# Second-norm tiles of six more blocks turned through DRAM, and images turned at the read in a transformer-block kernel

## The chip, the cores and the metric

The kernel runs on one core of a Trainium2 chip. The metric is device time in microseconds; three runs of the kernel before took 3532.73, 3537.45 and 3537.84 us, median 3537.45. A core has TensorE (PE, matmuls, with its weight loads shown apart as PEld), VectorE (DVE), ScalarE (ACT), GpSimd (POOL) and SyncE (SP). Nearly all DMAs of this kernel are issued by SP, in order, and are carried by sixteen DMA engines.

## The reference

One adaLN transformer block in float32 over x of shape (8, 1024, 512), 16 heads of 32, with a condition vector for each batch:

```python
mod = silu(condition) @ Wada + bada
sh_a, sc_a, gt_a, sh_m, sc_m, gt_m = split(mod, 6, axis=1)
xm = layernorm(x, g1, be1) * (1 + sc_a) + sh_a
x = x + gt_a * (causal_attention(xm, Wqkv) @ Wproj + bproj)
xm = layernorm(x, g2, be2) * (1 + sc_m) + sh_m
x = x + gt_m * (gelu(xm @ W1 + b1) @ W2 + b2)
```

W1 is 512 x 2048. The attention is causal over 1024 tokens.

## The kernel before

The 8 x 1024 tokens are cut into 16 blocks of 512: block n is half n % 2 of batch n // 2. Each block passes through: load and first norm (tile `hat_a`), the turned and modulated operand `xm_a` and its sums `t_a`, the projections k, q, v, attention, the output projection (`Wproj`), the second norm (`hat_m`, `xm_m`, `t_m`), and the MLP, `up` and `down`. The linear layers use a seven-product scheme of Strassen's kind, so that sums of operands and of weights are formed on DVE and POOL. All matmuls are float32 and go out as groups of four, one for each 32 columns of the array (`matmul`, L217). Weights come in 256 KB pieces through a ring of eight tiles `w` (`fetch`, L358 to L362), fetched ahead in the order of use.

**Windows.** `plan[w]` lists the linear steps that run beside the attention of block w: rest of the MLP of block w - 2, v of w, `proj` and `mt` of n = w - 1 (`mt` builds `xm_m` of n), then k, v or q of w + 1, then the first `up` products of n. So the second norm of an odd block n runs beside the attention of the even block n + 1.

**Attention.** Odd blocks, and the even ones up to 2, are attended with the keys along partitions: scores twice, exponentials from ACT, totals on POOL (L1854). The even blocks from 4 on are attended by rows (`attend_rows`), in ten units a block. In a unit, PE makes scores with queries along partitions, DVE takes maxima, ACT the exponentials `rows_p` (128 partitions x 2048 floats), and DVE turns every 32 x 32 piece of it. What is left is a permutation of whole 32-row bands, and that is done by DRAM: `spread_unit` writes the tile to a DRAM tile `image` (L2060) and reads it back as a page `turned` (L2076), from which PE multiplies with v (L2092). Raw tiles and pages share three SBUF slots. A unit's page is read when its image is written, a slot is free and the page before has been asked for.

**Turning a norm's tile.** `modulated` makes an operand with channels along partitions out of the normalized tile (tokens along partitions). For keys in the set `by_pe` PE transposes sixteen 128 x 128 pieces into PSUM banks (L778) and DVE or ACT move them out with gain and shift (L782, L788). For all others `turn` does as for images: DVE turns 32 x 32 pieces (L714), one 1 MB DMA writes `held` to DRAM (L723), four DMAs of 256 KB read it back into the tile (L728), and gain and shift are applied from SBUF. In the kernel before, `by_pe` holds the first norms of blocks 0 and 1 and the second norms of blocks 0, 1, 14, 15 and of 3, 5, 7, 9, 11 and 13. All `hat` tiles share one buffer.

**The order of work.** The program is written out as one static order for each engine by a planner in Python. It keeps model clocks (`now`), the time at which each thing will be there (`written`) and be free (`left`), and always goes on with the thread that waits least by these. DMAs are modelled by `note_dma(ns)`: 425 ns on SP for the issue, then 1000 ns until it begins or the end of the DMA before, then ns, then 1200 ns to land:

```python
        begun = max(now["SP"], due(reads, ()), after)
        now["SP"] = begun + ISSUE
        now["DMA"] = max(begun + BEGIN, now["DMA"]) + ns
        for k in writes:
            written[k] = now["DMA"] + LAND
```

At run time the engines wait on semaphores; the planner's times fix only the order. SP carries DMAs on eight semaphores in turn, and the rows below show it waiting for an earlier, unrelated DMA before it issues the next.

Of the kernel before, what the change touches and what calls it, by code (L numbers as in the profile page):

```python
# [9 lines left out]
F32 = mybir.dt.float32  # L10
# [12 lines left out]
def kernel(  # L23
# [33 lines left out]
    nc = tc.nc  # L57
    B, T, D = x.shape
    HD = W1.shape[1]
    P = 128  # L60
    hd = D // H
    scale = float(hd) ** -0.5
    TB = 512
    NTT = TB // P
# [18 lines left out]
    kept = ctx.enter_context(tc.tile_pool(name="kept", bufs=1, space=bass.MemoryType.DRAM))  # L83
# [7 lines left out]
    NB = len(blocks)  # L91
# [3 lines left out]
    written, left = {}, {}  # L95
# [9 lines left out]
    def due(reads=(), writes=()):  # L105
        t = 0.0
        for k in reads:
            t = max(t, written.get(k, 0.0))
        for k in writes:
            t = max(t, left.get(k, 0.0))  # L110
        return t

    def note(engine, ns, reads=(), writes=(), port=False):
        start = max(now[engine], due(reads, writes))
        if port:
            start = max([start] + [b for a, b in pool_spans if a <= start < b])
        end = start + ns
        now[engine] = end
        if engine == "POOL":
            pool_spans.append((start, end))  # L120
            del pool_spans[:-16]
        for k in reads:
            left[k] = max(left.get(k, 0.0), end + SYNC)
        for k in writes:
            written[k] = end + SYNC
        return end

    def note_dma(ns, reads=(), writes=(), after=0.0):
# [7 lines that stand above are left out]
    def note_pe(ns, form, reads=(), writes=()):  # L136
        now["PE"] = max(now["PE"], due(reads, writes))
        if shape[0] != form:
            shape[0] = form
            now["PE"] += SWITCH  # L140
        note("PE", ns, reads)
        spent[0] += ns
        for k in writes:
            written[k] = now["PE"] + PIPE
# [98 lines left out]
    def mlp_steps(n):  # L243
        return [("u", n, i) for i in range(NQ)] + [("d", n, part) for part in range(4)]
# [9 lines left out]
    for w in range(1, NB):  # L254
        n = w - 1
        m = mlp_steps(n)
# [29 lines left out]
    n = NB - 1  # L286
# [102 lines left out]
    rows = tmp.tile([P, TB], F32, tag="y", name="rows")[:n_rows, :P]  # L389
# [4 lines left out]
        r0 += n  # L394
    O_G1, O_BE1, O_G2, O_BE2, O_BPROJ, O_B2, O_B1, O_BADA = at

    by_pe = ({"a0", "a1", "m0", "m1", f"m{NB - 2}", f"m{NB - 1}"}) | {f"m{n}" for n in range(3, NB - 1, 2)}
    Q = P // NTT

    def hat_tile(key):  # L400
        return tmp.tile([P, NTT, D], F32, tag="hat", name=f"hat_{key}", bufs=1)

    def load_x(n):
        b, h = blocks[n]
        rows = hat_tile(f"a{n}")
        written["hat free"] = NEVER
        for t in range(NTT):
            some = x[b, h * TB + t * P : h * TB + (t + 1) * P, :]
            if f"a{n}" in by_pe:
                nc.sync.dma_start(rows[:, t, :], some)  # L410
            else:
                nc.sync.dma_start(rows[ts(t, Q), :, :], some.rearrange("(t i) d -> i t d", i=Q))
            note_dma(3600, [], [("x", f"a{n}")])
        return rows

    x_pre = {0: load_x(0)}
    fetch()

# [134 lines left out]
    def add_job(job, reads, first=False):  # L553

        at = sum(1 for other in jobs if other[2]) if first else len(jobs)
        jobs.insert(at, (job, reads, first))
# [149 lines left out]
    def turn(key, rows, xm):  # L706

        small_blocks = xm.rearrange("p c n -> p (c n)")
        by_tile = small_blocks.rearrange("p (m h t i) -> p h m t i", m=NTT, h=NC, t=NTT)
        written["blocks", key] = NEVER  # L710

        def turn_tile(t):
            into = by_tile[:, :, :, t, :]
            nc.vector.transpose(into, rows[:, t, :].rearrange("p (h m i) -> p h m i", m=NTT, i=Q))  # L714
            done = [("blocks", key)] if t == NTT - 1 else []
            note("DVE", 620, [("hat", key, t)], done)

        for t in range(NTT):
            add_job(lambda t=t: turn_tile(t), [("hat", key, t)], key[0] == "m")
        yield [("blocks", key)], []  # L720
        held = kept.tile([P, NTT * D], F32, tag=f"held_{turns[0] % 2}", name=f"held_{key}")
        turns[0] += 1
        nc.sync.dma_start(held, small_blocks)  # L723
        note_dma(2600, [("blocks", key)], [("held", key)])
        yield [("held", key)], []
        for m in range(NTT):
            some = held[:, ts(m, D)].rearrange("(a i) d -> i a d", i=Q)
            nc.sync.dma_start(rows[ts(m, Q), :, :], some)  # L728
            note_dma(1250, [("held", key)], [("turned", key)])
        yield [("turned", key)], []  # L730

# [3 lines left out]
    def modulated(key, gain, shift, b, guards):  # L735
# [23 lines left out]
        if turned:  # L759
            yield from turn(key, got, xm)  # L760
# [923 lines left out]
    def take_slot():  # L1684
        slot = free_p.pop(0)
        count_slots()
        return slot

    def give_slot(slot):
        free_p.append(slot)  # L1690
        count_slots()
# [362 lines left out]
    def spread_unit(n, raw, slot, parts, i):  # L2054

        yield [("p", slot)], []
        image = kept.tile([P, NTT, TB], F32, tag=f"image_{i % 5}", name=f"image_{n}_{i}")
        for a in range(NTT):
            into = image[:, a, :].rearrange("(b x) r -> x b r", x=hd)
            nc.sync.dma_start(into, raw[ts(a, hd)].rearrange("x (b r) -> x b r", b=NTT))  # L2060
            note_dma(700, [("p", slot)], [("image", n, i)])
        left["p", slot] = now["DMA"] + LAND
        written["image", n, i] += 1500
        raws.remove(slot)
        give_slot(slot)
        while True:
            yield [("image", n, i), SLOT, ("paged", n, i - 1)], []
            if free_p and len(pages) < 9:
                break
        taken_slot = take_slot()  # L2070
        pages.append(taken_slot)
        key = ("p", taken_slot)
        yield [], [key]
        written["paged", n, i] = 0.0
        page = pp.tile([P, NTT, TB], F32, tag=f"p{taken_slot}", name=f"turned_{n}_{i}")
        nc.sync.dma_start(page, image)  # L2076
        note_dma(2700, [("image", n, i)], [key])
        written[key] += 2000
        if i:
            yield [("valued rows", n, i - 1)], []  # L2080
        for qt, kh, c0, w, gg in parts:
            first = (n, gg) not in row_outs
            for k in range(w // P):
                yield [key, ("v", n), ("v done", n)], ["po"] if first and k == 0 else []
                if first and k == 0:
                    row_outs[n, gg] = [ps_po.tile([P, TB], F32, tag="o", name=f"po_{n}_{gg}"), 0]
                out = row_outs[n, gg]
                out[1] += 1
                for j in range(HPG):
                    r = slice(j * hd, (j + 1) * hd)  # L2090
                    at = c0 + k * P + j * hd
                    nc.tensor.matmul(  # L2092
                        out[0][r, ts(qt, P)],
                        vs[n][:, k, gg * P + j * hd : gg * P + (j + 1) * hd],
                        page[:, :, at : at + hd],
                        start=out[1] == 1,
                        stop=out[1] == 10,
                        skip_group_check=True,
                    )
                note_pe(2 * COLUMN * P, "columns", [key], ["po"])  # L2100
            if out[1] == 10:
                finish_rows(n, gg, out[0])
        pages.remove(taken_slot)
        give_slot(taken_slot)
        written["valued rows", n, i] = 0.0
# [27 lines left out]
    def finish_rows(n, g, out):  # L2133

        into = qTs[n][:, g, :]
        if wait_of(([("inverses", n, g)], [])) > 0 or max(now["DVE"], due(["po"])) > max(now["ACT"], due(["po"])) + 2500:
            nc.scalar.copy(into, out)
            note_act(585, None, ["po"], [("values", n, g)])
            start(scaled(n, g, into))
        else:  # L2140
            nc.vector.tensor_tensor(into, out, inverse_rows.pop((n, g)), ALU.mult)
            note("DVE", 690, ["po", "top"], [("att", n)])
            finished(n, g)
# [112 lines left out]
```

## Time and profile before

| | |
|---|---|
| median of three runs | 3537.45 us |
| profiled execution | 3537.05 us, span 3535.2 us |
| PE busy | 3398.7 us (96%) |
| DVE, POOL, ACT busy | 2287.1, 1790.1, 1249.8 us |
| DMA queue of SP | 603.15 MB, 55.7% of sixteen engines' span |
| images written / read | 240 DMAs of 256 KB / 60 of 1 MB |

In rows of groups stand line, engine, operation, tiles as out<-in, shapes and count, then busy time and the mean of one in ns, then idle time before it and what ended it. In rows of waits stand who waited for whom, the total in us, how many times, and the longest. In the chain and the timeline stand start and length in us. In rows of windows stand the busy times of the engines with their counts, then the granted share of PE's clock, the DMA share and GB/s. In rows of a DMA queue stand packets, MB and the share of sixteen engines.

### The profile page before, as it was taken

The numbers are of one execution on the slowest core, as the hardware profiler recorded it, in microseconds if no ns is written. First come the engines' busy times: TensorE is split into PE (matmuls) and PEld (weight loads), VectorE is DVE, ScalarE is ACT, GpSimd is POOL, SyncE is SP. The second block draws the span as 40 slices with busy tenths as digits, with TensorE's granted clock in tenths as the row PEclk, the third lists the DMA queues.
The fourth block names the chain that finished last, engine by engine and source line by source line (L and its number), as shares of the span: only waits on it lengthen the run. The fifth ranks groups of instructions, "written<-read, shape, count | busy, mean of one in ns | idle before, by whom it ended". The sixth has DMA issues, their size and how long they took to land.

```text
span 3535.2 us, 120275 instructions
## 1 busy us (share of the span) xinstructions
PE 3398.7 (96%) x53949; PEld 1726.5 (49%) x53949; DVE 2287.1 (65%) x2508; ACT 1249.8 (35%) x1878; POOL 1790.1 (51%) x1792
## 2 busy tenths in 40 slices
PE   8999999998999989999999999999999999999999
PEld 4444445454554545544454444544545445454455
DVE  5766675656667566675766657666667666576563
ACT  2334333252243522335323352323523334232421
POOL 3666846556038650476505764056730666308640
PEclk9999999999999999999999999999999999999999
DMA  6843434546755477553875548755487444863344
GB/s 199 262 149 112 139 94 137 149 113 209 231 187 155 115 236 222 182 152 109 262 234 166 146 116 266 235 159 145 134 280 219 140 141 159 276 200 110 96 134 140
DMA packets 373319, 610.88 MB, mean 173 GB/s; under 512 B 34748, under 2 KB 185084, under 8 KB 362308
## 3 DMA queue, kind: packets, MB, share of 16 engines
q1 hardware_dynamic: 372688, 603.15, 55.7%
q8 instruction: 425, 6.96, 0.8%
q14 instruction: 90, 0.74, 0.1%
q10 hardware_dynamic: 116, 0.03, 0.0%
HBM read 488.49 MB, written 112.46 MB: 170 GB/s over the span
## 4 chain that ended last, share of the span: by engine, by line
PE 78%; DVE 8%; DMA 6%; POOL 5%; issue 2%; SPq 1%; ACT 1%; ACTq 0%; DVEq 0%; POOLq 0%
PE bank L217 55%; PE sc L1613 6%; PE po L1760 5%; PE st L1719 5%; DMA turned<-image 3%; POOL pT L1854 3%; PE st L1707 2%; DVE mx L1628 2%; PE po L2092 2%; PE rows_sc L2017 1%; PE bank L1781 1%; DMA w<-in_L_cond_Wproj_dram 1%; DVE rows_max L2028 1%; DVE hT L167 1%; DVE sc L1625 1%
## 5 line engine op out<-in xcount | busy, mean ns | idle before, releaser
L1854 POOL TENSOR_TENSOR pT<-pT,pT 128x512 f32<-128x512 f32 (+3 forms) x966 | 1008.6, 1079 | 279.6 <-ACT pT L1732 230.1
L217 PE MATMUL bank<-w,hT 128*32 128x256 f32 x14336 | 824.3, 381 | 3.7 <-DVE hT L1226 2.9
L1732 ACT ACTIVATE pT<-st 128x2048 f32<-128x2048 f32 x228 | 428.3, 1879 | 749.5 <-PE st L1719 587.3
L1628 DVE TENSOR_REDUCE mx<-sc 128x4 f32<-128x2048 f32 (+3 forms) x287 | 522.8, 1839 | 243.0 <-PE sc L1613 239.6
L217 PEld LDWEIGHTS bank<-w,hT 128*32 128x32 f32 x14336 | 454.9, 110 | 388.0 <-issue 106.7
L217 PE MATMUL bank<-xm_m,w 128*32 128x256 f32 x8192 | 499.7, 381 | 0.0
L217 PE MATMUL bank<-t_m,w 128*32 128x256 f32 x6144 | 382.0, 380 | 8.2 <-DVE hT L208 8.2
L217 PEld LDWEIGHTS bank<-xm_m,w 128*32 128x32 f32 x8192 | 255.7, 110 | 218.5 <-issue 55.4
L2036 ACT ACTIVATE rows_p<-rows_sc,rows_minus 128x512 f32<-128x512 f32 (+3 forms) x384 | 196.8, 535 | 407.1 <-DVE rows_minus L2030 280.9
L217 PEld LDWEIGHTS bank<-t_m,w 128*32 128x32 f32 x6144 | 190.4, 110 | 181.9 <-issue 50.0
L1613 PE MATMUL sc<-kT,qT 32*128 32x512 f32 (+3 forms) x2296 | 262.1, 541 | 4.1 <-DVE mx L1628 2.4
L217 PE MATMUL bank<-w,qT 128*32 128x512 f32 x2048 | 245.1, 613 | 20.4 <-DMA w<-in_L_cond_Wproj_dram 19.5
L217 PE MATMUL bank<-xm_a,w 128*32 128x256 f32 x3968 | 245.8, 384 | 4.9 <-DVE u_q L208 2.2
L1760 PE MATMUL po<-pT,v 128*32 128x512 f32 (+3 forms) x2280 | 240.9, 513 | 7.1 <-POOL pT L1737 6.8
L1719 PE MATMUL st<-qT,kT 32*128 32x512 f32 (+3 forms) x2304 | 239.3, 505 | 0.0
L208 DVE TENSOR_TENSOR hT<-bank,u_u 128x512 f32<-128x512 f32 x183 | 122.7, 682 | 110.2 <-PE bank L217 102.5
L1737 POOL TENSOR_SCALAR_AFFINE_SELECT pT<-pT 128x512 f32<-128x512 f32 x160 | 117.9, 754 | 139.8 <-ACT pT L1732 139.8
L655 POOL TENSOR_SCALAR rstd_a<-mv_a 128x4 f32<-128x4 f32 x14 | 3.2, 230 | 363.2 <-DVE mv_a L634 362.8
L1625 DVE TENSOR_TENSOR sc<-sc,mask 128x1024 f32<-128x1024 f32 (+1 forms) x99 | 100.5, 1016 | 132.9 <-PE sc L1613 74.2
L217 PE MATMUL bank<-t_a,w 128*32 128x256 f32 x2944 | 185.3, 382 | 0.0
L217 PEld LDWEIGHTS bank<-xm_a,w 128*32 128x32 f32 x3968 | 127.6, 111 | 104.3 <-issue 23.0
L1129 ACT ACTIVATE hT<-hT,cols 128x512 f32<-128x512 f32 x256 | 164.8, 712 | 32.9 <-DVE hT L208 18.1
(270 smaller groups left out, 4149.7 us busy)
## 6 DMA issues: line engine op xcount, KB each, us to landing
w<-in_L_cond_W_dram SPq DMA_DIRECT2D x384, 256.0 KB
w<-kept_up_S SPq DMA_DIRECT2D x256, 256.0 KB
w<-kept_down_S SPq DMA_DIRECT2D x256, 256.0 KB
image<-rows_p SPq DMA_DIRECT2D x240, 256.0 KB
turned<-image SPq DMA_DIRECT2D x60, 1024.0 KB
w<-kept_qkv_S SPq DMA_DIRECT2D x180, 256.0 KB
w<-in_L_cond_Wqkv_dram SPq DMA_DIRECT2D x147, 256.0 KB
hat_a<-in_x_dram SPq DMA_DIRECT2D x64, 256.0 KB
```

The costliest lines, as they stand in the source:

```text
L208: nc.vector.tensor_tensor(out, src, other, op)
L217: nc.tensor.matmul(ps[r, :], columns, rhs, start=start, stop=stop, skip_group_check=True)
L1129: nc.scalar.activation(hT[:, i, :], hT[:, i, :], AF.Gelu, bias=cols[:, O_B1 + f : O_B1 + f + 1])
L1613: nc.tensor.matmul(sc[:, j, c0 : c0 + w], qTs[n][r, gg, ts(qt, P)], keys_of(n, kh)[r, gg, :w], start=True, stop=True, skip_group_check=True,)
L1625: nc.vector.tensor_tensor(place, place, shape_of.to_broadcast(place.shape), ALU.add)
L1628: nc.vector.tensor_reduce(maxima[n, gg][:, kh, qt, :], sc[:, :, c0 : c0 + w], axis=AX.X, op=ALU.max)
L1719: nc.tensor.matmul(st[:, j, c0 : c0 + w], kT[r, gg, ts(k % NTT, P)], qT[r, gg, TB - w :], start=False, stop=True, skip_group_check=True,)
L1732: nc.scalar.activation(pT[:, :, :used], st[:, :, :used], AF.Exp, scale=scale)
L1737: nc.gpsimd.affine_select(diagonal, diagonal, pattern=[[0, HPG], [1, P]], compare_op=ALU.is_ge, fill=0.0, base=0, channel_multiplier=-1,)
L1760: nc.tensor.matmul(po[r, TB - w :], v[:, k % NTT, g * P + j * hd : g * P + (j + 1) * hd], pT[:, j, c0 : c0 + w], start=(k == 0), stop=last ...
L1854: nc.gpsimd.tensor_tensor(into, into, pT[:, j, c0 : c0 + w], ALU.add)
L2036: nc.scalar.activation(tile_of[:, j], sc[:, j, c0 : c0 + w].rearrange("p (k b x) -> p k b x", b=NTT, x=hd), AF.Exp, bias=minus[:, i, j : j ...
```

## The change

Four edits.

- `by_pe` loses the second norms of blocks 3, 5, 7, 9, 11 and 13. These tiles now go through `turn`, and `down` reads their `hT` in the order of tokens that this leaves.
- The load of a first norm's tile (`load_x`) and the read back in `turn` keep their bytes and their four DMAs of 256 KB, but each DMA now fills all 128 partitions, 2 KB each, instead of 32 partitions with four rows of 2 KB.
- An image is written as it lies, by one DMA of 1 MB over 128 partitions instead of four of 256 KB from 32 partitions each, and the bands are permuted at the read: four DMAs of 256 KB, each into all 128 partitions, instead of one of 1 MB.
- The planner counts one write of 2600 ns instead of four of 700, four reads of 690 instead of one of 2700, and adds 3000 ns instead of 2000 to the time at which a page is expected.

```diff
-    by_pe = ({"a0", "a1", "m0", "m1", f"m{NB - 2}", f"m{NB - 1}"}) | {f"m{n}" for n in range(3, NB - 1, 2)}
+    by_pe = {"a0", "a1", "m0", "m1", f"m{NB - 2}", f"m{NB - 1}"}
...
-            some = x[b, h * TB + t * P : h * TB + (t + 1) * P, :]
             if f"a{n}" in by_pe:
-                nc.sync.dma_start(rows[:, t, :], some)
+                nc.sync.dma_start(rows[:, t, :], x[b, h * TB + t * P : h * TB + (t + 1) * P, :])
             else:
-                nc.sync.dma_start(rows[ts(t, Q), :, :], some.rearrange("(t i) d -> i t d", i=Q))
+                some = x[b, h * TB : (h + 1) * TB, :].rearrange("(m a i) d -> a m i d", a=NTT, i=Q)
+                nc.sync.dma_start(rows[:, t, :], some[t])
...
-        for m in range(NTT):
-            some = held[:, ts(m, D)].rearrange("(a i) d -> i a d", i=Q)
-            nc.sync.dma_start(rows[ts(m, Q), :, :], some)
+        for a in range(NTT):
+            some = held[ts(a, Q), :].rearrange("i (m d) -> m i d", m=NTT)
+            nc.sync.dma_start(rows[:, a, :], some)
             note_dma(1250, [("held", key)], [("turned", key)])
...
-        image = kept.tile([P, NTT, TB], F32, tag=f"image_{i % 5}", name=f"image_{n}_{i}")
-        for a in range(NTT):
-            into = image[:, a, :].rearrange("(b x) r -> x b r", x=hd)
-            nc.sync.dma_start(into, raw[ts(a, hd)].rearrange("x (b r) -> x b r", b=NTT))
-            note_dma(700, [("p", slot)], [("image", n, i)])
+        image = kept.tile([P, NTT * TB], F32, tag=f"image_{i % 5}", name=f"image_{n}_{i}")
+        nc.sync.dma_start(image, raw)
+        note_dma(2600, [("p", slot)], [("image", n, i)])
...
-        nc.sync.dma_start(page, image)
-        note_dma(2700, [("image", n, i)], [key])
-        written[key] += 2000
+        for a in range(NTT):
+            nc.sync.dma_start(page[:, a, :], image[ts(a, hd)].rearrange("x (b r) -> b x r", b=NTT))
+            note_dma(690, [("image", n, i)], [key])
+        written[key] += 3000
```

## The prediction

> **What bounds the kernel now.** I read the page's busy times first, then TensorE's waits, then busy time by stage.
>
> ```profile
> span 3535.2 us, 120275 instructions
> PE 3398.7 (96%) x53949; PEld 1726.5 (49%) x53949; DVE 2287.1 (65%) x2508; ACT 1249.8 (35%) x1878; POOL 1790.1 (51%) x1792
> PE po L2092 <- DMA turned<-image: 40.9, 18, 7.9
> PE bank L217 <- DMA w<-in_L_cond_Wproj_dram: 19.5, 6, 5.5
> PE st L1707 <- DVE mx L1628: 8.9, 11, 3.2
> ```
>
> TensorE (PE) is busy for 96% of the span and idle for 3535.2 - 3398.7 = 136.5 us. Two of its waits are for transfers and make up 60.4 us of that; the third is already small. So time can come from two places: work taken off PE, and these two waits.
>
> The stages are the windows in which a block is attended by rows (blocks 4, 6, ... 14; first row block below), against the windows between them (last row: their sum).
>
> ```profile
> 817.00:1012.00 195.00, 173.96 (x2856) 94.66 (x2856) 139.13 (x161) 62.86 (x169) 46.86 (x44) 0.94 0.74 229
> 1250.00:1455.00 205.00, 186.31 (x3116) 100.38 (x3112) 146.25 (x167) 65.05 (x172) 50.68 (x47) 0.97 0.75 235
> 1685.00:1878.00 193.00, 182.02 (x3116) 101.12 (x3117) 142.83 (x161) 64.19 (x171) 51.71 (x46) 0.99 0.81 250
> 2108.00:2312.00 204.00, 192.09 (x3276) 107.33 (x3272) 145.44 (x164) 65.55 (x173) 49.44 (x43) 0.98 0.80 246
> 2531.00:2736.00 205.00, 195.12 (x3296) 109.79 (x3296) 140.65 (x163) 67.72 (x174) 55.19 (x49) 0.98 0.78 243
> 2957.00:3175.00 218.00, 206.56 (x3548) 114.48 (x3548) 152.28 (x168) 67.67 (x174) 57.68 (x49) 0.98 0.76 238
> sum 1220.00, PE 1136.04 PEld 627.75 DVE 866.58 ACT 393.03 POOL 311.56; mean PE 189.34 PEld 104.63 DVE 144.43 ACT 65.51 POOL 51.93
> sum 1498.00, PE 1479.00 PEld 712.33 DVE 900.54 ACT 570.03 POOL 973.61; mean PE 246.50 PEld 118.72 DVE 150.09 ACT 95.01 POOL 162.27
> ```
>
> Columns: window, length, busy PE, weight load, DVE, ACT, POOL, then PE's granted clock, DMA share, GB/s. The six row windows hold 1220 - 1136 = 84 us of PE's idle time; the DMA engines are 0.74 to 0.81 busy there, and the clock drops to 0.94 where PE idles most. Lost clock: 195 x 0.06 + 205 x 0.03 + 193 x 0.01 + (204 + 205 + 218) x 0.02 = 32 us at most, part of it the windows' own starts. The change works in these six windows: the second norms of blocks 3, 5, ... 13 run beside blocks 4, 6, ... 14, whose pages are the image transfers.
>
> **Term 1, the turns taken off PE.** The same six windows, with the normalized tile of the second norm alone (PE's transposes, 16 a window):
>
> ```profile
> sum 1220.00, PE 17.73 PEld 10.80 DVE 5.47 ACT 9.83; mean PE 2.96 PEld 1.80 DVE 0.91 ACT 1.64
> ```
>
> 96 transposes leave, 17.7 us of a bound engine: -17.7. What they free besides (a bank four times a block) I cost at nothing. In their place come 24 DVE block transposes and, per block, one 1 MB write and four 256 KB reads.
>
> ```profile
> L714 DVE STREAM_TRANSPOSE xm_m<-hat_m 128x512 f32<-128x512 f32 x24 | 14.8, 675 | 0.0
> 1096.66 2.48 DVE L714 STREAM_TRANSPOSE xm_m<-hat_m 128x512 f32<-128x512 f32 x4
> 1102.52 0.37 SPq L723 DMA_DIRECT2D held_m<-xm_m  x1
> 1107.73 1.75 SPq L728 DMA_DIRECT2D hat_m<-held_m  x4
> 1116.57 1.00 DVE L782 TENSOR_SCALAR xm_m<-hat_m,gainm,shiftm 128x512 f32<-128x512 f32 x2 [0.36 <-DMA w<-in_L_cond_Wqkv_dram]
> 1120.39 1.76 DVE L800 TENSOR_TENSOR t_m<-xm_m 128x512 f32<-128x512 f32 x1 [2.10 <-ACT xm_m L788]
> 1781.19 0.33 PE L778 MATMUL bank<-ident,hat_m 128*128 128x128 f32 x1
> 1810.21 1.48 PE L217 MATMUL bank<-xm_m,w 128*32 128x256 f32 x24
> ```
>
> 24 x 0.675 = 16 us more DVE, 2.7 us in a window where DVE is 144 of 203 us busy: free while that slack stands; if DVE is late in it, up to 2.7 us a block. On SyncE (SP) the five issues take 0.37 + 1.75 us, and it waits for the write in between (5.2 us from one issue to the next). Behind it are weight pieces, pages and stores; the ring of eight weight tiles covers this, and without that cover it is up to 5 us a block.
>
> The chain of an even block (block 4, above) runs 1120.39 - 1096.66 = 23.7 us from the first DVE turn to the last operand's sum. Block 7, the tightest odd block, has 1810.21 - 1781.19 = 29.0 us from its first turn to `up`'s first matmul, and PE will be there about 3 us sooner: 26 us against 23.7. Bounds: nothing late, or late as the slowest chain of this kind in a loaded window (first rival, below); I take +4 over six blocks.
>
> **Term 2, the form of the transfers.** Three stretches, by packets, MB and share of sixteen engines: 24.6 to 30.2 us (a tile loaded over 128 partitions), 2372.9 to 2380.6 (four reads into 32 partitions each, with weights), 2367.5 to 2372.9 (a 1 MB write from 128 partitions).
>
> ```profile
> q1 hardware_dynamic: 887, 1.62, 90.9%
> q1 hardware_dynamic: 861, 1.32, 79.6%
> q1 hardware_dynamic: 144, 1.05, 48.2%
> ```
>
> Engine time per MB: 0.909 x 5.6 x 16 / 1.62 = 50 us over 128 partitions; 0.796 x 7.7 x 16 / 1.32 = 74 us, and with the 1.32 - 1.05 = 0.27 MB of weights in it at 50, 80 us for the 32-partition reads; 0.482 x 5.4 x 16 / 1.05 = 40 us for the large write. An image costs about 80 + 40 now (four writes from 32 partitions, one large read) and 40 + 50 after: 30 us, 1.9 us of all sixteen engines. Ten units, and the load and turn of one attention tile (80 to 50 twice), give 19 + 4 us a window; the new round trip takes (40 + 50) / 16 = 6 back. The DMA load in the row windows falls by 17 of some 157 us.
>
> The Trainium skill, "SBUF — State Buffer", section "Door 1: The DMA port swizzle", has a range of 32 partitions reach 8 of the 16 ports. By it the 32-partition form would cost 100 us per MB, an image would save 50 instead of 30, and term 2 would come to some -48; the trace's 80 is between the two forms' equal cost and that.
>
> How long the parts take now:
>
> ```profile
> 860.13 3.83 SPq L2060 DMA_DIRECT2D image<-rows_p  x4
> 862.62 5.75 DMA image<-rows_p
> 868.89 5.53 DMA turned<-image
> 874.46 1.94 PE L2092 MATMUL po<-turned,v 128*32 128x128 f32 x32 [7.92 <-DMA turned<-image]
> 1747.35 10.01 DMA turned<-image
> 1072.50 0.32 SPq L723 DMA_DIRECT2D held_a<-xm_a  x1
> 1076.46 1.75 SPq L728 DMA_DIRECT2D hat_a<-held_a  x4
> ```
>
> An image is on its way from 860.13 to 862.62 + 5.75 = 868.37, 8.2 us; the 1 MB write was out in 1076.46 - 1072.50 = 4.0 us at most, in a quiet window. I take 2.5 us saved. The read takes 5.5 us alone and 10.0 among others. Four reads over 128 partitions are in no row of their own: the tile load above fits into its 5.6 us with 0.6 MB beside it, the slow form has 8.8 us at most (1107.73 to 1116.57). I take 6, nearest to the 128-partition window: as now when alone, and shorter among others, since less is ahead of it in the queue.
>
> The order's side: one read of 2700 with 2000 added was expected 1000 + 2700 + 1200 + 2000 = 6900 ns after its issue, four of 690 with 3000 added are expected after 1000 + 2760 + 1200 + 3000 = 7960. So each page's matmuls are put 1.1 us later behind other work. With a read that is no longer, and about 1 us shorter under load, that takes some 2 us off waits of 40.9 / 18 = 2.3 us on average. The long ones stay in part: I leave 21 of the 40.9: -20 (bounds: -41 and, by rival (c), +20).
>
> The wait for the projection's weights:
>
> ```profile
> 2162.13 7.31 DMA hat_a<-held_a
> 2169.51 4.63 DMA w<-in_L_cond_Wproj_dram
> 2174.18 6.19 PE L217 MATMUL bank<-w,qT 128*32 128x512 f32 x32 [4.20 <-DMA w<-in_L_cond_Wproj_dram]
> ```
>
> SP could issue these weights only once the read of the turned attention tile before them had landed. At 50 for 80 us per MB that read ends some 2.5 us sooner, so most of the 19.5 us goes: -12 (0 to -19.5).
>
> **Term 3, the clock.** Stalls and lost clock stand in the same windows. With half of the stalls gone I take -12 of the 32 (0 to -32).
>
> **Sum.** -17.7 - 20 - 12 - 12 + 4 = -57.7. Where a stall goes, another is next: DVE's maxima (8.9 us above) and the page after it. I give +6 back: -52. The profiled execution took 3537.05 us (span 3535.2 and 1.85 around it), 0.4 under the median of the three runs, 3537.45. 3537 - 52 = **3485 us**.
>
> **Rivals.** (a) Slower: the new round trip lands after PE needs it. In a loaded window the attention tile's chain is longer:
>
> ```profile
> 1719.29 1.24 DVE L714 STREAM_TRANSPOSE xm_a<-hat_a 128x512 f32<-128x512 f32 x2
> 1756.26 0.69 DVE L800 TENSOR_TENSOR t_a<-xm_a 128x512 f32<-128x512 f32 x1
> ```
>
> 37 us, against 26 in block 7: 11 us late, in a place where nothing in the order expects it, since it plans 1000 + 2600 + 1200 ns for the write and 1000 + 5000 + 1200 for the reads, 12 us in all. At 11 us in each of six blocks, 66 us, and clock lost behind it, the gains of 58 are outweighed: 3545 to 3555. It decides from some 10 us a block on. Against it: DVE turned that tile in two pieces, 10 us apart, and the second norm's come first among DVE's jobs; and its transfers were in the slow form.
>
> (b) The transfers' form hides: pages wait for a free slot or for SP, not for bytes. Then only term 1 counts, with the +4: 3537 - 14 = 3523.
>
> (c) No change: four reads cost more than one. Had they the slow form's 8.8 us, a page would come 8.8 - 5.5 - 1.1 = 2.2 us later than the order expects against now, 18 x 2.2 = 40 us where the read now takes 5.5 and nothing where it takes 10; half of that, +20, with term 1 and the +4 makes 3537 - 17.7 + 20 + 4 = 3543, and 3537 with half of what I give for the weights. The Trainium skill, "DMA: Bandwidth & Descriptors", section "Measured (HBM→SBUF, 128 partitions, SWDGE, issued from GpSimd)", asks for batches of at least 1 MiB, and so speaks for this one. The window from 24.6 us, 1.6 MB in 256 KB pieces at 91% of the engines, speaks against it.
>
> **Numbers.** Forecast 0.60 (its own range 3455 to 3512), (b) 0.20, (a) 0.14, (c) 0.06. Three runs of this kernel lie within 0.15%, so 0.2%, 7 us, is about what tells from no change. Faster: the forecast and nearly all of (b), 0.79; same: most of (c) and the edges of its neighbours, 0.06; slower: (a) and the rest of (c), 0.15. Range 3455 to 3541: below the forecast's own low end and above (c) about 2 in 10 are left out, most of it (a).
>
> **What would show it.** Term 1: 64 transposes of the second norm on PE instead of 160, PE busy near 3380. Term 2: fewer than 55% of DMA share on the queue, PE's wait for pages near 20 us, for the projection's weights under 8. Term 3: a clock of 0.96 or more in the first row window. Wrong if `up`'s first matmuls wait for the second norm's tile, if pages' waits stay at 40 us, or if a wait that is small now (maxima, slots, DVE) takes their place.

## The result, and the profile after

| | before | after |
|---|---|---|
| median, four runs each | 3536.19 us | 4151.85 us |
| profiled execution | 3537.05 us, span 3535.2 | 4158.46 us, span 4156.7 |

The ratio is 1.1744 (95% interval 1.1724 to 1.1765): the kernel became 17.4% slower, 616 us, where 3485 us and a range of 3455 to 3541 had been forecast.

The page after, its span, busy times and the DMA queue of SP (packets, MB, share of sixteen engines):

```profile
span 4156.7 us, 120294 instructions
PE 3525.7 (85%) x53853; PEld 1797.3 (43%) x53853; DVE 2310.3 (56%) x2541; ACT 1255.5 (30%) x1884; POOL 1795.0 (43%) x1775
q1 hardware_dynamic: 372208, 615.71, 46.3%
```

The 96 transposes are gone (53949 - 53853). PE's idle time is 4156.7 - 3525.7 = 631.0 us against 136.5, so 494.5 more; PE is also busy for 127.0 us more, although it has less to do. The two make up the 621.5 us between the spans. The queue moves 2% more bytes and is busy for a smaller share, 46.3 instead of 55.7%. Most of that fall is the longer span: 0.463 x 4156.7 = 1925 us of all sixteen engines, against 0.557 x 3535.2 = 1969 before. So the kernel became slower while its DMA engines had no more to do.

PE's waits after:

```profile
PE po L2091 <- DMA turned<-image: 332.4, 45, 15.4
PE bank L217 <- DMA w<-in_L_cond_Wproj_dram: 30.7, 5, 11.1
PE bank L217 <- ACT xm_m L788: 27.1, 5, 7.0
PE sc L1613 <- ACT pT L1732: 24.0, 4, 8.3
PE bank L217 <- DMA w<-kept_qkv_S: 23.5, 3, 11.8
PE po L2091 <- DVE v L208: 15.8, 1, 15.8
```

The wait for pages went from 40.9 us to 332.4, from 18 times to 45, from 7.9 us at the longest to 15.4. That is 291.5 of the 494.5 us. The other rows grew, too: the waits for the modulated second norm (27.1) and for the weights `kept_qkv_S` (23.5) have no row before, and the one for the projection's weights was 19.5.

The stages in which even blocks are attended by rows, as windows (same columns as in the prediction):

```profile
841.00:1126.00 285.00, 186.71 (x2872) 103.89 (x2872) 152.55 (x173) 59.01 (x165) 50.07 (x48) 0.83 0.50 167
1381.00:1661.00 280.00, 195.37 (x3000) 108.15 (x2996) 153.12 (x172) 59.56 (x165) 52.87 (x47) 0.84 0.53 173
...
3481.00:3798.00 317.00, 222.19 (x3492) 122.62 (x3488) 154.19 (x169) 68.52 (x176) 57.26 (x48) 0.85 0.52 169
sum 1743.00, PE 1233.26 PEld 684.74 DVE 906.96 ACT 391.31 POOL 324.31; mean PE 205.54 PEld 114.12 DVE 151.16 ACT 65.22 POOL 54.05
```

The six windows grew from 1220 to 1743 us, 523 of the 621.5. In them PE is idle for 510 us instead of 84, and the granted clock is 0.83 to 0.86 instead of 0.94 to 0.99. The DMA share fell from 0.74 to 0.81 down to 0.50 to 0.57. So the place is the one that the prediction named, and the longest wait is for transfers, while DMA engines stand idle. That asks for a look at one transfer by itself. The timeline of a unit of block 14, when SP has nothing else to read:

```profile
3571.71 1.08 PE L2091 MATMUL po<-turned,v 128*32 128x128 f32 x32
3572.85 2.42 SPq L2075 DMA_DIRECT2D turned<-image  x4
3586.12 1.93 PE L2091 MATMUL po<-turned,v 128*32 128x128 f32 x32 [9.03 <-DMA turned<-image]
```

And the DMA queue in the ten microseconds from 3575 to 3585 within it (packets, MB, share), then windows of 5 us:

```profile
q1 hardware_dynamic: 493, 0.98, 25.9%
```

```profile
3575.00:3580.00 5.00, 2.08 (x20) 0.39 (x12) 3.43 (x4) 3.76 (x16) 1.26 (x1) 1.00 0.26 100
3580.00:3585.00 5.00, 0.00 (x0) 0.00 (x0) 0.00 (x0) 0.00 (x0) 0.00 (x0) 0.64 0.26 96
3585.00:3590.00 5.00, 3.88 (x44) 2.17 (x48) 0.00 (x0) 0.00 (x0) 0.00 (x0) 0.50 0.04 11
```

The four reads of a page take 3586.1 - 3572.9 = 13.2 us, where the prediction took 6. All the while the share is 0.26, about what four busy engines of sixteen make. Per MB that is 0.259 x 10 x 16 / 0.98 = 42 us of engine time, even a little less than the 50 that the prediction counted. That fits engines that are each as fast as it was thought, of which only a quarter carry the read. In the same three windows the clock goes from 1.00 to 0.50 while PE waits, and the page's matmuls then run at half speed.

The group of the pages' matmuls in the page after; before, at L2092, it was 287 ns for one and 45.0 us of idle time:

```profile
L2091 PE MATMUL po<-turned,v 128*32 128x128 f32 x1920 | 108.1, 385 | 385.9 <-DMA turned<-image 332.4 <-DVE v L208 15.8 <-issue 12.2
```

What the new reads have in common is how their source in DRAM begins. `"x (b r) -> b x r"`, `"i (m d) -> m i d"` and `some[t]` of `"a m i d"` all run slowest over a dimension of 4. The small transfers before began with 32, and the loads of a tile in plain order begin with 128. The Trainium skill has a rule for this, in "DMA: Bandwidth & Descriptors", section "Why a DMA increments its semaphore by 16 and not by 1": the slowest dimension longer than 1 of source and of destination decides, and the DMA is spread over the largest number of engines up to 16 that divides both. By it these reads get 4. The share of 0.26 agrees, and the experiments vary that dimension.

### The profile page after: what moved, and what is told of

It is laid out like the page before. It is cut to its first block, busy times and chain, and to the rows that moved or that the text cites. A ratio compares the mean times of both kernels' runs of the same rounds, so it can differ in the third digit from the quotient of the medians.

```text
span 4156.7 us, 120294 instructions
## 1 busy us (share of the span) xinstructions
PE 3525.7 (85%) x53853; PEld 1797.3 (43%) x53853; DVE 2310.3 (56%) x2541; ACT 1255.5 (30%) x1884; POOL 1795.0 (43%) x1775
## 3 DMA queue, kind: packets, MB, share of 16 engines
q1 hardware_dynamic: 372208, 615.71, 46.3%
## 5 line engine op out<-in xcount | busy, mean ns | idle before, releaser
L217 PE MATMUL bank<-w,hT 128*32 128x256 f32 x14336 | 837.0, 384 | 11.5 <-DMA w<-in_L_cond_W_dram 4.4
L217 PE MATMUL bank<-xm_m,w 128*32 128x256 f32 x8192 | 518.8, 392 | 42.8 <-ACT xm_m L788 27.1
L2091 PE MATMUL po<-turned,v 128*32 128x128 f32 x1920 | 108.1, 385 | 385.9 <-DMA turned<-image 332.4
L217 PEld LDWEIGHTS bank<-xm_m,w 128*32 128x32 f32 x8192 | 265.0, 113 | 275.7 <-issue 70.8
L217 PE MATMUL bank<-w,qT 128*32 128x512 f32 x2048 | 252.5, 626 | 31.6 <-DMA w<-in_L_cond_Wproj_dram 30.7
L2091 PEld LDWEIGHTS po<-turned,v 128*32 128x32 f32 x1920 | 79.8, 153 | 421.8 <-issue 324.4
L217 PE MATMUL bank<-xm_a,w 128*32 128x256 f32 x3968 | 256.0, 397 | 2.5 <-DVE xm_a L782 1.2
L1760 PE MATMUL po<-pT,v 128*32 128x512 f32 (+3 forms) x2280 | 243.4, 517 | 10.2 <-ACT top_rec L1794 5.8
L217 PE MATMUL bank<-t_a,w 128*32 128x256 f32 x2944 | 204.2, 414 | 41.2 <-DMA w<-kept_qkv_S 22.9
```

The costliest lines, as they stand in the source:

```text
L217: nc.tensor.matmul(ps[r, :], columns, rhs, start=start, stop=stop, skip_group_check=True)
L1760: nc.tensor.matmul(po[r, TB - w :], v[:, k % NTT, g * P + j * hd : g * P + (j + 1) * hd], pT[:, j, c0 : c0 + w], start=(k == 0), stop=last ...
L2091: nc.tensor.matmul(out[0][r, ts(qt, P)], vs[n][:, k, gg * P + j * hd : gg * P + (j + 1) * hd], page[:, :, at : at + hd], start=out[1] == 1 ...
```

## The experiments

The expectations name theories by letters. E is the number of engines, set by the slowest dimension of a read's source. Its rivals explain the loss by something else in the change: F by SP's queue and four DMAs in place of one, S by strided reads from DRAM, N by the moved norms or by the order, which expects pages later. All ratios are to the kernel before on the same chip, with a 95% interval.

### The slowest dimension 16, 8 and 128 (`s16_all`, `s8_all`, `nat_all`)

All three start from the kernel after and keep its order, its tiles, its DMAs' number and bytes. Only the source patterns of the three kinds of read change.

```diff
# s16_all (s8_all: s=8)
-nc.sync.dma_start(page[:, a, :], image[ts(a, hd)].rearrange("x (b r) -> b x r", b=NTT))
+some = image[ts(a, hd)].rearrange("x (b r) -> (x b) r", b=NTT)
+nc.sync.dma_start(page[:, a, :], some.rearrange("(y s) r -> s y r", s=16))
...
# the read back in turn and load_x: the same, "(y s) d -> s y d"
# nat_all: without the second rearrange, so that 128 rows of 2 KB lie in plain order
```

> The changed kernel with one thing different: in the 256 KB reads (pages, the read back of a turned tile, the load of a first norm's tile) the 128 pieces of 2 KB are taken from DRAM in another order, so that the source's slowest dimension is 16 long instead of 4; count, bytes, destination partitions, program order and waits are the changed kernel's. The permutation is then wrong, so this kernel leaves the right arrangement of tokens out. Theory E (engines: a DMA whose source pattern begins with a dimension of 4 is carried by 4 of the 16 DMA engines): the four reads of a page take 5 to 6 us instead of 13 to 23, PE's wait for pages falls from 332 us to under 30, time 3480 to 3520 us. Rival F (four reads on SP's queue and eight semaphores cost more than one): time stays above 4000 us. Rival S (strided reads from DRAM are slow): stays above 4000 us, its source being strided too. Rival N (the second norms that moved to DRAM, or the later order of pages): above 3900 us.

> As s16_all with the slowest dimension 8 long, again without the right arrangement. Theory E: 8 of 16 engines, a page's four reads some 7 to 8.5 us, time between the others and nearer to the fast one, 3520 to 3650 us. Rivals F, S and N: no difference from the changed kernel, above 4000 us.

> The changed kernel with its 256 KB reads taken from DRAM in plain order (128 rows of 2 KB one after the other, both patterns beginning with 128); the arrangement of tokens is then wrong, as in s16_all, whose source had the same length of the slowest dimension from the engines' view but steps of 32 KB. Theory E alone (sixteen engines are all that matters): as s16_all, 3545 to 3560 us. Rival S2 (the steps in DRAM cost the rest): reads of 5 to 6.5 us instead of 8.4, time 3500 to 3530 us.

Measured: `s8_all` 3711.93 us, 1.0489 (1.0459 to 1.0519); `s16_all` 3555.54 us, 1.0048 (1.0033 to 1.0063); `nat_all` 3501.76 us, 0.9906 (0.9891 to 0.9920). A page alone, from the timeline of each, its first issue and the matmul that waited for it (the row of issues runs on into the next page's), with PE's wait for pages and the queue's share in the middle of that read (3191 to 3195 in the first, 3050 to 3052.5 in the second). `s8_all`:

```profile
3188.62 11.86 SPq L2076 DMA_DIRECT2D turned<-image  x6
3197.45 1.78 PE L2092 MATMUL po<-turned,v 128*32 128x128 f32 x32 [4.60 <-DMA turned<-image]
```

```profile
PE po L2092 <- DMA turned<-image: 107.4, 35, 10.9
```

```profile
q1 hardware_dynamic: 370, 0.71, 50.4%
```

`s16_all`:

```profile
3047.76 10.47 SPq L2076 DMA_DIRECT2D turned<-image  x8
3054.65 1.08 PE L2092 MATMUL po<-turned,v 128*32 128x128 f32 x32 [2.66 <-DMA turned<-image]
```

```profile
PE po L2092 <- DMA turned<-image: 47.4, 23, 9.1
PE bank L217 <- DMA w<-in_L_cond_Wproj_dram: 2.6, 2, 2.0
```

```profile
q1 hardware_dynamic: 298, 0.55, 75.2%
```

`nat_all`:

```profile
3005.61 9.76 SPq L2071 DMA_DIRECT2D turned<-image  x8
3012.12 1.46 PE L2087 MATMUL po<-turned,v 128*32 128x128 f32 x32 [2.28 <-DMA turned<-image]
```

```profile
PE po L2087 <- DMA turned<-image: 25.3, 15, 7.9
```

| slowest dimension of the source | 4 (after) | 8 | 16 | 128, plain |
|---|---|---|---|---|
| step from row to row of a page in DRAM, KB | 8 | 16 | 32 | 2 |
| queue's share during a lone read | 0.26 | 0.50 | 0.75, after a lull | (not in steady flow) |
| small packets of a lone read | 16 | 32 | 64 | 64 |
| four reads of a page alone, us | 13.2 | 8.8 | 6.9 | 6.5 |
| PE's wait for pages, us | 332.4 | 107.4 | 47.4 | 25.3 |
| time, us | 4152 | 3712 | 3556 | 3502 |

With the order and the DMAs held fixed, the source's pattern alone moves the time by 650 us, and the share doubles from 4 to 8 as E says. F and N fall as the cause of the 616 us: order, queue, the number of DMAs and the moved norms are the same in all four. S falls as well: the steps in DRAM grow from 8 to 32 KB while the loss goes away.

The packets count the engines more directly than the share does. SP's queue over the whole of `s8_all`, `s16_all` and `nat_all`:

```profile
q1 hardware_dynamic: 373808, 615.72, 53.3%
q1 hardware_dynamic: 377008, 615.73, 57.2%
q1 hardware_dynamic: 377008, 615.73, 54.3%
```

For the same bytes these are 1600, 4800 and 4800 packets more than the 372208 after. The new form is that of 400 DMAs (240 for pages, 104 in `turn`, 56 in `load_x`), so each has 4, 12 and 12 packets more. A lone read (3572 to 3588 in the kernel after, then 3188 to 3198, 3047 to 3057 and 3005 to 3013) shows them: 512 packets of 2 KB and, besides, 16, 32, 64 and 64 of under 512 bytes, which is 4, 8, 16 and 16 for each of its four DMAs. One for each engine is what E asks for. Counted from the packets' starts and durations, exactly four were under way for 8 of the 10 us from 3575 to 3585.

E's own numbers were off: `s16_all` came out above the range expected, and `s8_all` as well.

From 16 in strides of 32 KB to plain order it is still some 50 us (1.0048 and 0.9906), with sixteen engines in both, which E alone does not explain. The same four DMAs are on SP for longer where the source is strided. Issues of page reads, least, median and most in ns, in `s16_all` and `nat_all`:

```profile
L2076 SPq DMA_DIRECT2D turned<-image x240: 514/592/1713, 841.9 to 3187.3; - x120
```

```profile
L2071 SPq DMA_DIRECT2D turned<-image x240: 319/430/1746, 845.5 to 3138.5; - x120
```

For the same packets and bytes the engines are also busy for longer, 0.572 x 3553.1 = 2032 us of all sixteen against 0.543 x 3505.2 = 1903, so something besides the issue differs. How the 50 us divide between the issue and the strides in DRAM was not told apart.

### Which reads cost it (`page_only`, `turn_only`)

From the kernel before: `page_only` takes only the edits of `spread_unit` and of the page (with its +3000), `turn_only` only those of `load_x` and of the read back in `turn`; `by_pe` stays as before in both.

> The kernel before with the changed images alone: one write of 1 MB, four reads whose source begins with a dimension of 4, pages expected 3000 ns later. Loads, turned tiles and PE's turns as before. Theory E: most of the loss is here, since 60 of the 86 reads of 1 MB by four engines are pages and PE waits for each: 3900 to 4050 us.

> The kernel before with the changed form of the loads and of the read back of turned tiles alone (four engines for these 36 times 1 MB), images and PE's turns as before. Theory E: the first norms' tiles are needed a window later than they are read, so most of it hides; what shows is pages and weights in the queue behind them and behind SP's eight semaphores: 3570 to 3680 us.

Measured: `page_only` 4011.41 us, 1.1351 (1.1326 to 1.1376); `turn_only` 3623.25 us, 1.0253 (1.0230 to 1.0275). PE's waits, in `page_only` and in `turn_only`:

```profile
PE po L2091 <- DMA turned<-image: 304.1, 42, 15.5
```

```profile
PE bank L217 <- DMA w<-in_L_cond_Wproj_dram: 51.0, 5, 14.3
PE po L2092 <- DMA turned<-image: 45.3, 19, 8.5
```

The pages make 4011.4 - 3535.9 = 475 us, the loads and the turns that were there before 87 us, both within the range expected. In `turn_only` the pages' wait hardly moved; the wait for the projection's weights went from 19.5 to 51.0 us, since SP issues them behind the read of the turned attention tile. These two waits are 36 of the 87 us; the rest is in smaller ones and in PE's busy time. The expectations count 86 reads of 1 MB by four engines, and 36 without the pages; by the packets above there are 100, and 34 in `turn_only`. What is left of the 616, 53 us, belongs to the moved second norms with their reads in the slow pattern, or to the parts together; that split was worked out by difference and not run.

### Sixteen engines, but 32 partitions (`p32_all`)

The kernel after, with `load_x` and `turn` in their old form, and the page read band by band, which begins with 32 on both sides:

```diff
-for a in range(NTT):
-    nc.sync.dma_start(page[:, a, :], image[ts(a, hd)].rearrange("x (b r) -> b x r", b=NTT))
+for b in range(NTT):
+    some = image[:, ts(b, TB)].rearrange("(a x) r -> x a r", x=hd)
+    nc.sync.dma_start(page[ts(b, hd), :, :], some)
     note_dma(690, [("image", n, i)], [key])
```

> The changed kernel computed rightly, its reads in another cut: a page is read by four DMAs of 256 KB into 32 partitions each, whose patterns begin with 32 on both sides; the turned tiles and the loads have the form of the kernel before. The images are still written by one DMA of 1 MB, the second norms of the six blocks go through DRAM, pages are expected 3000 ns later. Theory E: sixteen engines at the slower rate of 32 partitions, a read of 8 to 9 us; time 3500 to 3570 us. Rival F: above 4000. Rival N: above 3900.

Measured: 3623.28 us, 1.0243 (1.0225 to 1.0260). Timeline of a page alone, then PE's wait for pages:

```profile
3103.64 11.33 SPq L2076 DMA_DIRECT2D turned<-image  x8
3111.66 1.54 PE L2092 MATMUL po<-turned,v 128*32 128x128 f32 x32 [3.79 <-DMA turned<-image]
```

```profile
PE po L2092 <- DMA turned<-image: 78.4, 30, 9.7
```

The read takes 8.0 us, as expected, and lies between those of `s8_all` and `s16_all`, and so do the wait and the time; the time is above the 3570 expected. This is the form whose 8.8 us the prediction had as its upper bound. Against `m_only` (3547, below), which has the same norms and the old images, it is 76 us slower; so even the bound cost far more than the 20 us that rival (c) gave it. It keeps the permutation, and is still slower than the kernel before.

### The other parts alone (`m_only`, `traffic`, `m_free`, `late_only`, `one_one`, `nat_pe`)

`m_only` is the kernel before with the edit of `by_pe` alone. `traffic` keeps PE's transposes and adds the round trip beside them. `m_free` is `m_only` without that round trip. `late_only` is the kernel before with one number changed.

```diff
# traffic, after PE has turned m3, m5, ... m13
+start(there_and_back(key, got))   # one write of 1 MB, four reads of 256 KB, only the tile's next user waits
# m_free, on top of m_only: in turn, after DVE's turns, for m3, m5, ... m13 alone
+written["turned", key] = written["blocks", key]
+return
# late_only
-written[key] += 2000
+written[key] += 3000
```

> The kernel before with the one edit of the set of tiles turned by PE: the second norms of blocks 3, 5, ... 13 go through DRAM, in the form of transfers before. PE is spared 17.7 us. Theory E with term 1 of the prediction: 3515 to 3535 us. Rival (a) of the prediction (the tile comes late in a loaded window): 3545 to 3560 us, with PE's first matmuls of up waiting for the tile. Rival N: above 3700.

> The kernel before, PE's turns kept, with the moved norms' transfers added as a dead weight: after PE has turned the second norm of blocks 3, 5, ... 13, its tile is written to DRAM (1 MB) and read back in place by four DMAs into 32 partitions each. Nothing waits for them but the next user of the tile. If the gain of 17.7 us in m_only was eaten by traffic and SP's queue: 3550 to 3562 us, with a wait for pages near 48 us. If it was eaten by the tile's lateness or by DVE's turns: 3535 to 3545 us.

> m_only without the transfers: for the second norms of blocks 3, 5, ... 13 DVE turns the pieces and the tile is then used as it lies in SBUF, with no trip through DRAM (arrangement wrong). PE is spared the 96 transposes, DVE has its 24, no traffic, no lateness. If term 1 was right in itself: 3515 to 3525 us. If DVE's turns or the free slots on PE eat it: 3530 to 3545 us.

> The kernel before with pages expected 3000 ns after their modelled landing instead of 2000, nothing else. By the prediction, page matmuls behind 1 us more of other work: PE's wait for pages falls by 10 to 15 us, time 3522 to 3532 us. Rival: the order moves the wait elsewhere, 3535 to 3550 us.

Measured: `m_only` 3547.23 us, 1.0024 (1.0010 to 1.0038); `traffic` 3548.32 us, 1.0037 (1.0022 to 1.0051); `m_free` 3528.24 us, 0.9975 (0.9961 to 0.9989); `late_only` 3539.17 us, 1.0005 (0.9994 to 1.0016). The busy times and PE's waits in `m_free`:

```profile
PE 3383.1 (96%) x53853; PEld 1734.7 (49%) x53853; DVE 2276.4 (64%) x2507; ACT 1263.6 (36%) x1900; POOL 1787.6 (51%) x1794
PE po L2095 <- DMA turned<-image: 61.6, 24, 8.0
```

PE's 96 transposes free 3398.7 - 3383.1 = 15.6 us of its time, close to the 17.7 forecast. But its wait for pages grows by 20.7 us and its idle time as a whole by 10.2 (3529.8 - 3383.1 = 146.7), and some 9 us of the time are left as gain (0.25%). The round trip alone costs 11 us (`traffic`), and the edit as made is a loss of 8 (`m_only`). The 9 and the 11 would leave a loss of 2; the order that the planner writes also differs between these kernels, and the rest stays open. PE's wait for pages in `traffic`, then the one in `m_only` with that for the second norm:

```profile
PE po L2105 <- DMA turned<-image: 39.9, 23, 7.3
PE po L2092 <- DMA turned<-image: 48.5, 22, 8.0
PE bank L217 <- ACT xm_m L788: 3.7, 2, 2.3
```

So the time of `m_only` is that of rival (a), but not by its mechanism, for PE waits 3.7 us for the second norm. Nor does `traffic` cost by the wait for pages, as was expected: that wait is 39.9 us, as before. Both `traffic` and `m_free` came out between the two ranges expected for them.

In `late_only` the wait that the number aims at does fall, from 40.9 to 27.1 us, others take part of its place, and the time does not change, as the rival there had it:

```profile
PE po L2092 <- DMA turned<-image: 27.1, 17, 7.7
PE st L1707 <- DVE mx L1628: 15.9, 16, 3.2
PE po L1760 <- POOL pT L1737: 7.7, 6, 2.4
```

The last two put the transfers' form to the test where all sixteen engines carry it. `one_one` is the kernel before with one 1 MB write and one 1 MB read for an image and no permutation between; `nat_pe` is `nat_all` with `by_pe` as before.

```diff
# one_one
+nc.sync.dma_start(image, raw)
...
-nc.sync.dma_start(page, image)
+nc.sync.dma_start(page.rearrange("p a r -> p (a r)"), image)
```

> The kernel before with an image written by one DMA of 1 MB and read by one of 1 MB, no permutation between (left out, so the result is wrong); all else as before. It is the most that a better form of the image transfers could bring. By the prediction's term 2 (a write 2.5 us shorter, less traffic): PE's wait for pages falls from 41 to some 20 us, time 3500 to 3520 us. Rival (b) of the prediction (pages wait for slots and for SP, not for bytes): 3530 to 3542 us.

> nat_all with the second norms of blocks 3, 5, ... 13 turned by PE again (arrangement wrong as there). If the moved norms gain nothing even with the fast form of transfers: 3490 to 3503 us, as nat_all or below. If term 1 holds once the transfers are fast: 3512 to 3522 us, nat_all being 17.7 us less.

Measured: `one_one` 3525.10 us, 0.9969 (0.9957 to 0.9981); `nat_pe` 3509.17 us, 0.9936 (0.9916 to 0.9957). PE's wait for pages in `nat_pe`:

```profile
PE po L2087 <- DMA turned<-image: 30.9, 16, 7.2
```

Both came out between the ranges expected. So a large write in place of four slow ones, with the order that follows from it, is worth some 12 us, and all transfers over 128 partitions with sixteen engines some 23 us, both without the permutation. Beside `nat_pe`, `nat_all` shows the moved norms as a gain of 0.3% when their round trip is fast, where in `m_only` they were a loss of 0.24%; the two intervals of `nat_pe` and `nat_all` touch, so that sign is likely and not settled.

A read with the right permutation, 128 partitions and sixteen engines was not tried.

## Why the prediction was wrong, step by step

- **The step that failed** stands in term 2, the form of the transfers: "Four reads over 128 partitions are in no row of their own: ... I take 6". They take 13.2 us. The window it was priced by shows loads whose source lies in plain order, 128 rows after one another; the new reads have the same destination and the same pieces of 2 KB, but a source that begins with 4. The engine time per MB, on which the step rests, was right (42 measured for 50), and dividing it by sixteen engines was wrong: four carried the read. The upper bound, 8.8 us in the slow form, was a bound on the destination's form only. "-20" on pages became +291.5 in the waits and 475 us in the time.
- **The weights of the projection**, "-12": 30.7 us instead of 19.5, by the same cause, since the tile's read that they queue behind is one of the new ones. With sixteen engines the step holds: 2.6 us in `s16_all`, where under 8 was forecast.
- **Term 3**, the clock, went the other way. It was tied to the stalls, rightly: at 0.83 to 0.86 in the row windows, PE's busy time rose by 127 us instead of falling.
- **Term 1**: the count was right (64 transposes on PE, 15.6 us off PE's busy time in `m_free` for 17.7). As a term of the sum it was worth 9, for the freed time runs into the wait for pages, and the round trip, costed at 6 us of the DMA load and nothing on the path, takes 11 back by `traffic`. Term 1 together with its "+4" came out as +8 by `m_only` instead of -14.
- **The order**, 3000 instead of 2000: counted as part of the 20 us, it is worth nothing by itself (`late_only`).
- **The rivals.** (c) had the right place and the right sign, four reads that cost more than one, with a chance of 0.06 and a price of 20 us; the slow form costs 76 (`p32_all` against `m_only`), the form with four engines 475. (a) spoke of a late second norm; that wait is 27.1 us after, a part of the whole, and 3.7 in `m_only`, where the reads are the old ones. (b), the form is hidden, is refuted: with all else held fixed the form moved the time by 650 us. None of the three had a price above 3555. The -48 in term 2 is not worked out there; its -32 (-20 and -12), scaled by 50 for 30, would be -53.
- **The signs named.** Fewer than 55% of DMA share came true, 46.3%, and had been named as a sign of success. It fell because the span grew and because the new reads left twelve engines without work, so it told nothing of a gain. "If pages' waits stay at 40 us" was the right alarm, and so was the wait of `up` for the second norm.
- **What was right in it**: with the reads spread over sixteen engines in plain order, and so without the permutation, the change is worth 0.94%, some 33 of the 52 us (`nat_all`). No kernel here has that speed with the right permutation.

## What to carry to other kernels

Before a transfer is priced from a row, compare the whole pattern on both sides, above all the slowest dimension of the source: here 4, 8 and 16 in that place gave 98, 178 and, with a lull in the window, 220 GB/s (0.98 MB in 10 us, 0.71 in 4, 0.55 in 2.5). A low DMA share while someone waits for a DMA asks for a look at one transfer alone; a share near 4/16 or 8/16 there, and 4 or 8 small packets for a DMA, named the cause here. A wait on the critical path cost about its whole length: a read 7.7 us longer than in one of 1 MB (13.2 for 5.5) came to 475 us over 60 pages, 7.9 a page. Part of that is the clock, which the waits brought down: PE was busy for 127 us more in the kernel after.

## What was not expected of the hardware

- Four DMAs together, issued one after another on one queue, did not reach more than 26% of the engines: the next DMA of the same kind did not use the engines that the first left idle (0.26 in each of two windows of 5 us, 493 packets).
- A wait of PE of 9 us, from 3577.1 to 3586.1, brought the granted clock down: by windows of 1 us it was 1.00 up to 3581, 0.71 in the next and 0.50 from 3582 on. It stayed at 0.50 for the first 4.9 us of work after the wait, up to 3591. Before, these stages ran at 0.94 to 0.99.
- SP's issue of a 256 KB read took 430 ns (median) with a source in plain order and 592 ns with one in strides of 32 KB.
- With the engines equal, reads of 128 rows in plain order and in strides of 32 KB differ by 1.4% of the whole kernel (0.9906 and 1.0048 of the kernel before).
